# A hybrid block (linear attention, FFN, softmax attention, FFN) on one core: loads ahead, two products moved to ScalarE, weight codes converted early, down projections and softmax reordered

## The chip, the cores and the metric

The kernel runs on 1 core of one Trainium2 chip. The metric is device time in microseconds of one execution; smaller is better. A core has five engines with a queue each: TensorE (PE, matrix products), VectorE (DVE), ScalarE (ACT), GpSimd (POOL) and SyncE (SP, which here issues nearly all DMAs). In the profile PEld is PE's loading of stationary operands.

## The reference

All arithmetic is float32. `x` is 2 x 1024 rows of 512. Four residual sublayers follow each other:

```python
x = x + linear_attention(layernorm(x))   # 4 heads of 128, chunks of 128 rows
x = x + ffn(layernorm(x))
x = x + softmax_attention(layernorm(x))  # one head of 512, W_q, W_k, W_v, W_o
x = x + ffn(layernorm(x))                # the same weights again
```

The FFN's weights are int32 codes: `W = (code - 128) * scale[:, None]`, 1408 hidden units, and its value is `down(silu(gate(x)) * up(x))`.

The linear attention, for each chunk of 128 rows and each head:

```python
k = k / max(norm(k), 1e-12); alpha = sigmoid(x @ Walpha + b); beta = softplus(x @ Wbeta + b)
cla = cumsum(log(alpha + 1e-6))                      # inside the chunk
decay = where(causal, exp(cla - cla.T), 0)
y_local = ((q @ k.T) * beta.T * decay) @ v
y_glob = (q @ state.T) * exp(cla)
kw = k * beta * exp(cla_end - cla)
state = state * exp(cla_end) + v.T @ kw              # carried from chunk to chunk
```

Its output is `y_local + y_glob`.

## The kernel before

**Precision.** Most operands are kept as a pair: a rounded "high" part (format float32r) made by ScalarE and the remainder, the "low" part, made by VectorE (sometimes POOL). This is `split` (lines 83 to 86). A product of two pairs is three matmuls, `mm3` (95 to 98). Matmuls are 128x128 stationary by up to 512 columns; results go to eight PSUM buffers.

**Order.** The program is written as one straight list of instructions. A planner (`schedule_with_timeline_sim`) then places them on the engines by a simulated timeline of its own; the written order is the priority, not the final order. Each engine executes its own list strictly in the order planned. `behind(instructions)` (76 to 81) forbids the planner to place what is inside the block ahead of the given instructions on the same engine. Tiles come from pools; a pool with `bufs=2` has two buffers for a name, and a third use waits until the first is free. The large pool is `slots`, twelve buffers of 8 KB a partition (`slot`), which hold weights, transposed activations and FFN operands in turn.

**Start.** A weight product M = Wq Wk^T of the softmax attention is made in four steps (`weight_product`), while the first four tiles of x (128 rows each) are normed and transposed by PE (`ln_tile`): none at step 0, tile 0 at step 1, tiles 1 and 2 at step 2, tile 3 at step 3. Each tile's load is issued inside `layernorm` (103 to 117). Then Wq, Wk and Wv are loaded through four stage buffers and split (`load_wqkv`).

**Linear attention loop.** For t = 0 to 15: one head of the q projection of four tiles further on (`q_head`), k and v projections of tile t+1 (`kv_tile`), the decay matrix of tile t+1 (`decay`: load a row of cumulated logs broadcast to all partitions, mask on POOL, four exponentials on ACT, L491), then `scores(t)`: transpose k, normalise the next k (`k_norm`, which also makes kw on POOL, L531), decay the state (POOL, L555), add to it, form the output of tile t-1 (`chunk_out`) and the scores of t, multiply with the decay matrix (`at`, L566). Beside this, `fill[t]` holds layer norm steps for later tiles: for the attention's tiles 8 to 15 and for the FFN's first 8 tiles (nm "f"). A step of `ln_steps` is either `ln_norm` (norm a tile, transpose blocks of 32 on VectorE into y) or `ln_move` (four DMAs that put the blocks in place). In the loop's last tiles the operands of a second weight product V = Wv Wo are loaded and split, the product is made, and `combine` forms the seven operands of the first FFN pass.

**FFN.** Gate and up projections are done together as a 2x2 block product with seven multiplications, P1 to P7 (`products`, L304), in 2 passes of 8 tiles, each with 11 steps j of 128 hidden units. The stationary operands of a step are eight 128x256 blocks (`stationary`): gate and up codes and four sums or differences of them. In the very first pass they are made from the codes: load, convert to float on ACT (`codes`, L271), four sums on POOL (287 to 290), and seven of the eight blocks are written to DRAM as `wc`; later passes load them from there. The down codes are converted in the attention loop (`down_weights`). `finish(j)` applies silu and the product and splits the hidden values of tiles 0 and 1 of the pass.

After the 11 steps come eight down projections (i = 0 to 7, 22 matmuls each, L761 and 762). Their stationary operand hs is a pair for each tile, from a pool of two buffers; tile i+1 is split while tile i is multiplied (`h_split`). The result is scaled on VectorE (L763) and the residual is added on POOL (L765; on VectorE only for the very last tile). In the blocks behind, norm steps or `combine` steps for the next pass or stage are taken.

**Softmax attention.** For two batches of 8 tiles: `scores_b(i+1)` (maximum on VectorE L829, its negative nm L832 and L833, exponential on ACT L838), `probs_T(i)` (transpose on VectorE, to DRAM and back in four DMAs, then split into pth and ptl), `out_b(i-1)`. The last tile is transposed on PE instead (ppt, L866). `fill[b][i]` again holds norm and combine steps for the next stage.

Of the kernel before, what the change touches and what calls it, by code (L numbers as in the profile page):

```python
# [22 lines left out]
H = 4  # L23
# [11 lines left out]
def hybrid_block_kernel(ctx: ExitStack, tc: tile.TileContext, a, out):  # L35
# [67 lines left out]
    def layernorm(src, name, tag="xin"):  # L103

        xin = xp.tile([P, D], F32, tag=tag, name=f"xin_{name}")
        nc.sync.dma_start(out=xin, in_=src)
        bn = mp.tile([P, 6], F32, tag="bn", name=f"bn_{name}")
# [6 lines left out]
        nc.gpsimd.tensor_tensor(rs, ve, mhalf, ALU.pow)  # L114
# [4 lines left out]
    def layernorm_T(src, xT, i, name, tag="xin"):  # L119

        xn = layernorm(src, name, tag)
# [19 lines left out]
    wc_d = [dp.tile([P, 7, 256], F32, tag=f"wc_{j}", name=f"wc_{j}") for j in range(KH)]  # L141
# [29 lines left out]
    def spill(pool, tag, ps, dst, name):  # L171
        for m in range(KD):
            hi, lo = (pool.tile([P, 512], F32R, tag=tag, name=f"{name}{m}_{j}") for j in range(2))
            split(hi, lo, ps[m])
            nc.sync.dma_start(out=dst[m][:, 0:512], in_=hi.bitcast(F32))
            nc.sync.dma_start(out=dst[m][:, 512:1024], in_=lo.bitcast(F32))

    lnT, lnY = {}, {}

    def ln_norm(src, nm, st, i):  # L180


        if i == 0:
            lnY[nm, st] = yp.tile([P, 4, KD, ST, 32], F32, tag="y", name=f"y_{nm}{st}")
        t = st * ST + i
        xn = layernorm(src[t], f"{nm}{t}")
# [78 lines left out]
    def codes(pool, tag, dst, src_ap, name):  # L265

        c = pool.tile([P, 512], I32, tag=tag, name=name)
        nc.sync.dma_start(out=c, in_=src_ap)
        if len(dst.shape) == 3:
            c = c.rearrange("p (n c) -> p n c", n=2)  # L270
        nc.scalar.activation(dst, c, AF.Identity, bias=zero)  # L271

    def down_weights(sp, j):
        c = sp.tile([P, 512], F32, tag="stg", name=f"cf{j}")
        codes(sp, "stg", c, a["wd"][j], f"cd{j}")
        nc.sync.dma_start(out=wd_d[j], in_=c)

    def stationary(j, name, fresh=None):
# [3 lines left out]
        if fresh:  # L282
            a21, a11, s1, s2, s3, a12, s4, a22 = (w[:, n] for n in range(8))
            codes(*fresh, w[:, 1:6:4], a["wgu"][j][:, 0:512], f"cg{name}_{j}")
            codes(*fresh, w[:, 0:8:7], a["wgu"][j][:, 512:1024], f"cu{name}_{j}")
            f = lambda x: x.bitcast(F32)
# [4 lines left out]
            nc.sync.dma_start(out=wc_d[j], in_=f(w[:, 1:8]))  # L291
        else:
            nc.sync.dma_start(out=w[:, 1:8].bitcast(F32), in_=wc_d[j])
# [728 lines left out]
```

## Time and profile before

| | us |
|---|---|
| median of 3 runs | 997.01 (995.41 to 999.16) |
| the profiled execution, its own time | 995.43 |
| its span, first to last instruction | 993.7 |
| PE busy (4450 matmuls) | 955.3, 96% |
| DVE busy | 681.8, 69% |
| ACT busy | 374.2, 38% |
| POOL busy | 269.0, 27% |
| DMA: 160.06 MB | mean 161 GB/s |
| mean granted PE clock | 0.991 |

The profile is one execution seen by the hardware profiler. Busy time of PE is a pipelined figure, so an engine at 96% is waiting for at least the rest. Its groups name the line of the kernel, the engine, the output and input tiles with buffer numbers left out, the shape, and what ended the engine's idle time before them. Stages in the span: start to 30 us; attention loop to 252; first FFN, passes to 325 and 455 with their down projections after them, to 500; softmax attention to 760; second FFN to the end.

### The profile page before, as it was taken

Reading aid. Unit: us, or ns where it says so; the run is one execution under the profiler, and the core shown is the slowest. Engines: PE = TensorE matmul, PEld = TensorE weight load, DVE = VectorE, ACT = ScalarE, POOL = GpSimd, SP = SyncE. Lnnn points to the kernel's source line nnn. Section 1 sums busy time; section 2 is a strip of 40 time slices with the busy share of each in tenths; the row PEclk is TensorE's granted clock in tenths of the full one; section 3 lists DMA queues with packets and bytes.
Section 4 is the critical chain, followed back from the end, with each engine's and each line's share of the span. In section 5 each row is a group of like instructions: output and inputs, shape, how many; then the busy total and the mean of one; then the engine's idle time right before and its main releaser. Section 6 shows DMA issues by size and latency. Waiting matters only on the chain.

```text
span 993.7 us, 13137 instructions
## 1 busy us (share of the span) xinstructions
PE 955.3 (96%) x4450; PEld 786.8 (79%) x4450; DVE 681.8 (69%) x1294; ACT 374.2 (38%) x719; POOL 269.0 (27%) x345
## 2 busy tenths in 40 slices
PE   8999999988898999999999999999997999999998
PEld 6788888877776777887888888888876888788877
DVE  7666858779876699786526556356667775976665
ACT  4653334233665433443222223222223443444421
POOL 4442314253634133212200411205501111321122
PEclk9999999999999999999999999999998999999999
DMA  8536364564797555652704767328668762464112
GB/s 271 200 104 174 124 156 140 142 180 158 253 350 229 148 202 205 185 146 75 264 22 88 163 162 168 98 64 190 165 151 271 250 175 44 152 235 153 38 53 96
DMA packets 219250, 160.06 MB, mean 161 GB/s; under 512 B 154992, under 2 KB 170672, under 8 KB 219184
## 3 DMA queue, kind: packets, MB, share of 16 engines
q1 hardware_dynamic: 217136, 155.03, 52.3%
q0 software_dynamic: 2048, 4.20, 2.0%
q8 instruction: 35, 0.57, 0.2%
q14 instruction: 31, 0.25, 0.1%
HBM read 102.66 MB, written 41.84 MB: 145 GB/s over the span
## 4 chain that ended last, share of the span: by engine, by line
PE 56%; DVE 2%; SPq 2%; DMA 1%; ACT 1%; issue 1%; POOL 0%; ACTq 0%; DVEq 0%
PE pZg L304 4%; PE pXg L304 4%; PE pVg L304 4%; PE pog L762 4%; PE pog L761 4%; PE psc L96 3%; PE psc L98 3%; PE pob L96 3%; PE psc L97 3%; PE pob L97 3%; PE pob L98 3%; PE pYg L304 2%; PE pof L762 2%; PE pof L761 2%; PE pqb L97 1%; PE pqb L96 1%
## 5 line engine op out<-in xcount | busy, mean ns | idle before, releaser
L762 PE MATMUL pof<-wdf,hsf 128*128 128x512 f32 x176 | 68.3, 392 | 4.3 <-DVE hsf L86 4.3
L762 PE MATMUL pog<-wdg,hsg 128*128 128x512 f32 (+1 forms) x187 | 69.0, 378 | 3.0 <-DVE hsg L86 3.0
L761 PE MATMUL pog<-wdg,hsg 128*128 128x512 f32 (+1 forms) x187 | 69.1, 378 | 0.0
L761 PE MATMUL pof<-wdf,hsf 128*128 128x512 f32 x176 | 68.1, 391 | 0.0
L96 PE MATMUL pob<-vh,pth 128*128 128x512 f32 x128 | 50.8, 397 | 0.0
L96 PE MATMUL psc<-xh_b,qh 128*128 128x512 f32 x128 | 50.5, 395 | 0.0
L98 PE MATMUL psc<-xh_b,ql 128*128 128x512 f32 x128 | 50.5, 395 | 0.0
L97 PE MATMUL psc<-xT_b,qh 128*128 128x512 f32 x128 | 50.5, 394 | 0.0
L97 PE MATMUL pob<-vl,pth 128*128 128x512 f32 x128 | 50.5, 394 | 0.0
L98 PE MATMUL pob<-vh,ptl 128*128 128x512 f32 x128 | 50.4, 394 | 0.0
L304 PE MATMUL pXf<-B_f,wcf 128*128 128x512 f32 x176 | 47.0, 395 | 3.3 <-ACT u2f L729 2.2
L86 POOL TENSOR_TENSOR hsg<-sgg,hsg 128x128 fp32r<-128x128 f32 x40 | 17.6, 460 | 117.6 <-ACT hsg L85 95.4
L304 PE MATMUL pVf<-T_f,wcf 128*128 128x512 f32 x176 | 46.6, 391 | 1.4 <-DVE upf L735 0.7
L304 PE MATMUL pXg<-B_g,wcg 128*128 128x512 f32 x176 | 47.2, 389 | 0.0
L304 PE MATMUL pVg<-T_g,wcg 128*128 128x512 f32 x176 | 46.7, 389 | 0.0
L85 ACT CAST pth<-ptl 128x512 fp32r<-128x512 f32 x30 | 17.1, 619 | 75.9 <-DMA ptl<-p 64.0
L765 POOL TENSOR_TENSOR xrf<-of,xrf 128x512 f32<-128x512 f32 x16 | 25.0, 1562 | 75.3 <-DVE of L763 61.4
L838 ACT ACTIVATE pe<-psc,nm 128x512 f32<-128x512 f32 x32 | 21.7, 684 | 58.6 <-DVE nm L833 58.6
L762 PEld LDWEIGHTS pog<-wdg,hsg 128*128 128x128 f32 x187 | 35.1, 188 | 10.0 <-DVE hsg L86 3.6
L762 PEld LDWEIGHTS pof<-wdf,hsf 128*128 128x128 f32 x176 | 33.1, 188 | 12.6 <-DVE hsf L86 5.8
L304 PEld LDWEIGHTS pXf<-B_f,wcf 128*128 128x128 f32 x176 | 32.3, 188 | 12.8 <-ACT u2f L729 4.0
L765 POOL TENSOR_TENSOR xrg<-og,xrg 128x512 f32<-128x512 f32 x15 | 24.4, 1624 | 61.5 <-DVE og L763 48.7
(288 smaller groups left out, 2667.7 us busy)
## 6 DMA issues: line engine op xcount, KB each, us to landing
wcg<-wc SPq DMA_DIRECT2D x22, 896.0 KB, 5.8
wc<-wcf SPq DMA_DIRECT2D x11, 896.0 KB, 4.5
wcf<-wc SPq DMA_DIRECT2D x11, 896.0 KB, 4.8
p<-py SPq DMA_DIRECT2D x15, 512.0 KB, 3.0
ptl<-p SPq DMA_DIRECT2D x60, 128.0 KB, 3.0
xin_a<-in_x SPq DMA_DIRECT2D x16, 256.0 KB, 4.6
xra<-in_x SPq DMA_DIRECT2D x16, 256.0 KB, 3.0
row<-cl SPq DMA_DIRECT2D x16, 256.0 KB, 4.0
```

Of the source, the lines that this page charges most:

```text
L85: c = nc.scalar.copy(hi, src)
L86: return c.ins, (eng or nc.vector).tensor_tensor(lo, src, hi.bitcast(F32), ALU.subtract).ins
L96: nc.tensor.matmul(ps, lhs_hi, rhs_hi, start=first, stop=False)
L97: nc.tensor.matmul(ps, lhs_hi, rhs_lo, start=False, stop=False)
L98: return nc.tensor.matmul(ps, lhs_lo, rhs_hi, start=False, stop=last).ins
L304: nc.tensor.matmul(ps, w[:, m, k * P : (k + 1) * P], o[:, s, k, :], start=first and k == 0 and s == 0, stop=k == 1 and s == 1, skip_group_ ...
L761: nc.tensor.matmul(ps, hs[i][:, 0, j], wd[j][:, ds], start=j == 0, stop=False)
L762: nc.tensor.matmul(ps, hs[i][:, 1, j], wd[j][:, ds], start=False, stop=j == KH - 1)
L765: add.tensor_tensor(xr[:, ds], o[:, ds], xr[:, ds], ALU.add)
L838: nc.scalar.activation(pe[:, s * 512 : (s + 1) * 512], pS[s], AF.Exp, bias=nm, scale=SC, accum_out=rs[:, s : s + 1],).ins
```

## The change

**Loads ahead.** `load_x` is taken out of `layernorm`. The first four tiles are loaded at product steps 0 and 1, tiles 0 and 1 are normed at step 1, tiles 2 and 3 at step 2. Wq is loaded in step 2, into the buffer of y, and split from there, behind the latest inverse root on POOL. `ln_norm` loads the tile after its own too, within a group of four. The broadcast rows of `decay` are loaded up to two tiles ahead (`load_row`), and `decay(t+1)` comes after `scores(t)`.

**To ScalarE.** kw and the decayed state are made by four ACT instructions each, one a head, instead of one POOL instruction.

**Codes.** All 33 blocks of codes are loaded, converted on ACT and stored during tiles 0 to 11 (`convert`, called three times a tile; each call starts one load and converts and stores an earlier block). `stationary` then loads four blocks of float codes and forms (first pass) or loads (later) the other four; formed ones are stored. The first two stationaries are formed after the loop.

**Spread.** The norm steps for the FFN come earlier (tiles 6 to 11 instead of 6 to 12); the V operands at tiles 13, 14, 14 and 15 instead of 12 to 15; combine steps three each at tiles 12, 13 and 14, and the last three in the FFN's first step, behind the last spill of V. In the first FFN pass norm steps are taken in twos.

**Down projections and softmax.** hs of tile 2 gets two buffers of `slots` and is split around the last `finish`; from then on tile i+2 is split while tile i is multiplied. The residual add goes to VectorE. In `probs_T` the splits are put behind the latest exponential (ACT) and reciprocal (DVE).

```diff
-        nc.gpsimd.tensor_tensor(rs, ve, mhalf, ALU.pow)
+        rsqrt[:] = [nc.gpsimd.tensor_tensor(rs, ve, mhalf, ALU.pow).ins]
...
     def ln_norm(src, nm, st, i):
+        t = st * ST + i
+        for n in range(t, min(t + 2, st * ST + ST)):
+            if (nm, n) not in lnX:
+                lnX[nm, n] = load_x(src[n], f"{nm}{n}")
...
+    def load_codes(sp, n, j):
+        c = sp.tile([P, 512], F32, tag="stg", name=f"c{n}{j}")
+        src = {"g": a["wgu"][j][:, 0:512], "u": a["wgu"][j][:, 512:1024], "d": a["wd"][j]}[n]
+        nc.sync.dma_start(out=c.bitcast(I32), in_=src)
+        return n, j, c
+
+    def store_codes(n, j, c):
+        nc.scalar.activation(c, c.bitcast(I32), AF.Identity, bias=zero)
+        if n == "d":
+            nc.sync.dma_start(out=wd_d[j], in_=c)
+        else:
+            dst = wa_d[j][:, 1:3] if n == "g" else wa_d[j][:, 0:4:3]
+            nc.sync.dma_start(out=dst, in_=c.rearrange("p (n c) -> p n c", n=2))
+
+    def stationary(j, name, form=False):
         w = slot(f"wc{name}_{j}").rearrange("p (n c) -> p n c", n=8)
+        nc.sync.dma_start(out=f(w[:, 0:4]), in_=wa_d[j])
+        if form:
+            a21, a11, a12, a22, s1, s2, s3, s4 = (w[:, n] for n in range(8))
...
+            nc.sync.dma_start(out=ws_d[j], in_=f(w[:, 4:8]))
         else:
-            nc.sync.dma_start(out=w[:, 1:8].bitcast(F32), in_=wc_d[j])
+            nc.sync.dma_start(out=f(w[:, 4:8]), in_=ws_d[j])
...
-                weighted = nc.gpsimd.tensor_tensor(kw, kf, s2.unsqueeze(2).to_broadcast([P, H, P]), ALU.mult)
+                for h in range(H):
+                    weighted = nc.scalar.activation(kw[:, h, :], kf[:, h, :], AF.Copy, scale=s2[:, h : h + 1])
...
-                    nc.gpsimd.tensor_tensor(
-                        old, sta[t], ec[:, 2, i, :].unsqueeze(2).to_broadcast([P, H, P]), ALU.mult
-                    )
+                    for h in range(H):
+                        nc.scalar.activation(old[:, h, :], sta[t][:, h, :], AF.Copy, scale=ec[:, 2, i, h : h + 1])
...
+            if k < 2:
+                xs += [load_x(xa[t], f"a{t}", "xres" if t > 1 else "xin") for t in (2 * k, 2 * k + 1)]
+            if k == 2:
+                staged = yp.tile([P, 4, KD, ST, 32], F32, tag="y", name="y_Wq")
+                staged = staged.rearrange("p k a b c -> p k (a b c)")
+                for m in range(KD):
+                    wq_loaded = nc.sync.dma_start(out=staged[:, m], in_=a["Wq"][m * P : (m + 1) * P, :]).ins
             pm, end = next(prep)
             with behind((end, loads[-1][2])):
-                for t in ((), (0,), (1, 2), (3,))[k]:
+                for t in ((), (0, 1), (2, 3), ())[k]:
                     ln_tile(t)
...
-            (x1, "f", 0, (6, 7, 8, 9, 9, 9, 10, 10)),
-            (x1, "f", 1, (10, 10, 11, 11, 11, 11, 12, 12)),
+            (x1, "f", 0, (6, 6, 7, 7, 7, 7, 8, 8)),
+            (x1, "f", 1, (9, 9, 10, 10, 10, 10, 11, 11)),
...
+        def convert(t):
+            if t < 12 and taken:
+                if items:
+                    taken.append(load_codes(sp, *items.pop(0)))
+                store_codes(*taken.pop(0))
+
         for t in range(NT):
+            convert(t)
             if t + 4 < NT:
                 q_head(*divmod(t + 4, ST))
+            load_row(t + 1)
+            if (t + 2) % ST:
+                load_row(t + 2)
             if t + 1 < NT:
                 kv_tile(t + 1)
+            convert(t)
+            weighed = scores(t)
+            if t + 1 < NT:
                 decay(t + 1)
-            scores(t)
-            with behind(normed.get(t + 1, ())):
+            with behind(normed.get(t + 1, (weighed,))):
                 for step in fill[t]:
                     step()
...
+                for n in {NT - 3: (0,), NT - 2: (1, 2), NT - 1: (3,)}.get(t, ()):
+                    loads.append(product_operands(sp, a["WvT"], a["Wo"], "V", n))
+                for n in range(3 if t >= NT - 4 and t < NT - 1 else 0):
                     moving.pop(0)()
+                convert(t)
...
+        wcs = [stationary(n, "f0", True) for n in range(2)]
         chunk_out(NT - 1)
-        spill(a3, "state", next(prep)[0], vo_d, "V")
+        spilled = spill(a3, "state", next(prep)[0], vo_d, "V")
...
+                        if i == 2:
+                            two = [slot(f"hs{nm}{pr}_{i}{n}") for n in "hl"]
+                            hs[i] = [x[:, 0 : KH * P].rearrange("p (j c) -> p j c", j=KH) for x in two]
...
+                    with behind(behind_first if first and j < 2 else ()):
+                        while moving:
+                            moving.pop(0)()
+                        plan = (0, 2, 2, 2, 2, 0, 2, 2, 2, 0, 2) if first else (1, 1, 1, 1, 2, 2, 1, 1, 1, 1, 2)
+                        for _ in range(plan[j] if early else 0):
+                            early.pop(0)()
...
+                h_split(2, slice(0, KH - 1), ha[:, 0, 0 : KH - 1], None)
                 done = finish(*begun)
+                h_split(2, KH - 1, ha[:, 0, KH - 1], None)
...
-                    if 1 <= i < 2 * ST - 1:
-                        n = i + 1
+                    if 1 <= i < 2 * ST - 2:
+                        n = i + 2
...
-                        add = nc.vector if last else nc.gpsimd
-                        add.tensor_tensor(xr[:, ds], o[:, ds], xr[:, ds], ALU.add)
+                        nc.vector.tensor_tensor(xr[:, ds], o[:, ds], xr[:, ds], ALU.add)
...
-            for s in range(2):
-                ks = slice(s * 4, s * 4 + 4)
-                split(hi[:, ks], lo[:, ks], raw[:, ks])
+            with behind(last):
+                for s in range(2):
+                    ks = slice(s * 4, s * 4 + 4)
+                    split(hi[:, ks], lo[:, ks], raw[:, ks])
```

## The prediction

> **What bounds the kernel now.** I read the page first: part 1 says that TensorE (PE) is busy for 955.3 of 993.7 us, so no engine can be relieved to any profit unless PE waits for it. Then I cut the span into the kernel's stages and asked for busy time, granted clock and DMA share of each (columns: PE, PEld, DVE, ACT, POOL busy us with instruction counts, clock, DMA share, GB/s).
>
> ```profile
> 0.00:30.00 30.00, 26.03 (x111) 20.19 (x112) 22.00 (x52) 14.37 (x26) 13.82 (x24) 0.94 0.87 284
> 30.00:200.00 170.00, 169.44 (x962) 144.80 (x961) 120.09 (x301) 72.12 (x154) 55.64 (x64) 1.00 0.50 144
> 200.00:252.00 52.00, 43.40 (x250) 37.78 (x249) 46.22 (x99) 18.45 (x35) 25.03 (x25) 0.93 0.56 165
> 252.00:325.00 73.00, 66.39 (x278) 50.61 (x277) 54.60 (x103) 43.47 (x81) 35.76 (x46) 1.00 0.85 284
> 325.00:388.00 63.00, 59.45 (x258) 47.88 (x257) 50.58 (x75) 22.70 (x35) 16.58 (x14) 1.00 0.55 175
> ...
> 455.00:500.00 45.00, 43.53 (x192) 35.62 (x191) 27.04 (x30) 14.03 (x22) 11.64 (x8) 1.00 0.54 196
> ...
> 740.00:760.00 20.00, 13.21 (x53) 10.77 (x52) 19.28 (x37) 6.72 (x12) 1.83 (x3) 0.83 0.68 194
> ...
> 840.00:876.00 36.00, 34.53 (x152) 28.16 (x151) 29.93 (x29) 14.54 (x19) 9.76 (x6) 1.00 0.40 132
> ```
>
> The linear attention's steady part (30 to 200 us), the second halves of both FFN passes and the softmax attention up to 740 us are full: nothing is to be had there. All that can be won is PE's idle time in seven places: start 4.0 us, attention's tail 8.6, first FFN pass 6.6, down projections 3.5 + 1.5 + 1.5 + about 1.5 (at 957.6), softmax's end 6.8; about 34 us. A low clock adds to it: 0.06 of 30 us, 0.07 of 52, 0.17 of 20, that is 1.8 + 3.6 + 3.4 = 8.8 us. The ceiling of any reordering is thus some 43 us.
>
> PE's waits name what ends last in each (columns: total, times, longest):
>
> ```profile
> PE ppt L866 <- ACT pe L838: 6.8, 1, 6.8
> PE pof L762 <- DVE hsf L86: 4.3, 4, 1.5
> PE pl L578 <- DVE at L566: 3.2, 1, 3.2
> PE pd L549 <- POOL kw L531: 3.1, 2, 2.2
> PE pog L762 <- DVE hsg L86: 3.0, 2, 1.5
> PE pkT L540 <- DVE kb L524: 2.3, 3, 0.9
> PE pXf L304 <- ACT u2f L729: 2.2, 3, 0.8
> PE pab L365 <- ACT xh_a L85: 1.7, 1, 1.7
> ```
>
> The timeline shows why the down projections stall (the third tile's operand at 957 us, and a later tile's at 355 us):
>
> ```profile
> 957.47 1.27 POOL L765 TENSOR_TENSOR xrg<-og,xrg 128x512 f32<-128x512 f32 x1 [9.69 <-issue]
> 957.57 1.99 DVE L86 TENSOR_TENSOR hsg<-hag,hsg 128x768 fp32r<-128x768 f32 x1 [0.23 <-ACT hsg L85]
> ...
> 355.60 0.94 DVE L86 TENSOR_TENSOR hsf<-hbf,hsf 128x768 fp32r<-128x768 f32 x1
> ```
>
> The same instruction takes 0.94 us alone and 1.99 us when a POOL add runs beside it; and it can only start once tile 0's matmuls have freed one of the two hs buffers.
>
> **What the Trainium skill says.** "SBUF — State Buffer", section "Who interferes with whom": VectorE with two SBUF inputs and GpSimd reading SBUF exclude each other for the whole instruction, while ScalarE has ports of its own. The trace agrees: 1.05 us longer, about the length of the add. "TensorE: Matmul & The Clock Gate", section "Part 1: The HAM clock gate": an idle window of about 3.4 us halves the clock for at least another. The trace agrees in kind: the clock falls to half after the waits near 20, 206, 246 and 745 us, not after the 1.5 us ones; here waits of 2.2 and 3.2 us were already enough. For the price of a new operation, "ScalarE: Activation LUTs", section "What ACT_TABLE_LOAD costs": 280 ns and 0.833 ns an element with a pointer operand, less 93 ns back to back, so an estimate of 0.29 us for 128 columns; the trace's own row has four decays (L491, 128x128) in 1.28 us, 0.32 each, which I use.
>
> **The change, part by part**, against the profiled execution (995.4 us, span 993.7).
>
> *Start.* Four x tiles are loaded by name ahead and normed at product steps 1 and 2 instead of 1 to 3; Wq goes to the idle y buffer instead of waiting for stage buffers. Now tile 3's transposes end the M product (18.3 us) and PE then waits 1.7 + 0.9 us for its halves, after which 3.4 us run at half clock. With tile 3 done a step earlier both waits go. Eight loads of 256 KB now stand on SP's queue about the M operands, at 0.87 DMA share; a 1 us delay of an M operand is possible. Gain 2.6 + 1.7, less 1: **3.3** (0 to 4.5).
>
> *Steady loop.* kw (15 tiles) and the decayed state (14 tiles) leave POOL (1.13 and 1.04 us each) for ScalarE, four instructions of 0.32 each, 1.28 us: 29 x 1.28 = 37 us more ACT. The 22 gate and up code conversions (0.72 us) leave the FFN for tiles 0 to 11: 15.8 us. Of this some 13 x 2.56 + 15.8 = 49 us falls in 30 to 200, on top of 72.1: 121 of 170 us, 71%. ACT is in order, so kT, qT and the squares may stand behind a group of four. PE has projections to run meanwhile. SP gets 22 loads and 22 stores more at 0.33 to 0.43 us, some 1.5 us in a tile of 12 us, and DMA 11.5 MB more, 68 GB/s on 144; the rows, now loaded up to two tiles ahead, are out of reach of that. A store waits for its conversion, and behind it wait x loads and x1 stores. From nothing to 1.5 us a tile; I take a **loss of 3** in all.
>
> *Attention's tail.* Here DVE is 46.2 of 52 us busy: it is the bound, not PE. What goes: f's norms of tiles 4 to 7, each 0.68 + 0.17 + 0.14 + 0.55 + 0.65 = 2.2 us, move a tile or so earlier, so about two tiles' worth leaves the window (4.4); three of the twelve combining steps go behind the last spill (about 3.5); with kw and the decayed state off POOL, port blocks like the 2.06 us for a 1.21 us B_f split at 227 us shrink (say 3 us). Forming two stationaries (8 x 0.8 us of POOL) moves past the loop's end; kw's two waits (3.1) go, for ScalarE is two fifths busy here. DVE falls to about 35 of 52. That removes perhaps two thirds of 8.6 and one of two slow-clock windows: **7** (3 to 11).
>
> *First FFN pass.* ACT loses 22 conversions that stood in its queue ahead of u2 and waited for code loads (8.1 + 2.3 us by the waits). Instead weights come by DMA: load 512 and store 512 KB a step against 512 and 896 before, on queues 0.85 busy. POOL still forms 4 x 0.8 = 3.2 us a step of 6.3. Norm steps are two at a time, same total. PE's waits here were u2, sg, wcf: **5** of 6.6 go (2 to 6.5).
>
> *Down projections.* hs of tile 2 gets two slots of its own and is split before or right after the last finish; each later tile is split two ahead. The start waits have no cause left. The residual add goes to DVE: 0.68 us more a tile of 5 us, against a 1 us block removed. If no block was there, DVE in 340 to 388 rises from 39.8 to at most 45.2 of 48: still covered, but the second pass's operands, combined there on DVE, would come later (0.9 us wait at 386.7 now). Of 8.0 us idle: **6.5** (3 to 8).
>
> *Softmax's end.* The splits of tile 14's probabilities are put behind tile 15's exponentials. Before, ACT took pth at 748.1 when its DMA landed, DVE took ptl between the two nm steps (747.9 and 750.6), and the exponentials came at 751.1. Without these, nm is done near 748.1 and exponentials follow T_g's casts, at 748 to 749.5: 2.3 us. What is late next is DVE: the maxima stand behind combining steps until 744.9, though scores ended at 739.7, and that stays. One slow-clock window of two may go, 1.7: **4** (0 to 9). Elsewhere in the stage the new wait only orders ACT and DVE, which are a quarter and a half busy.
>
> Sum: 3.3 + 7 + 5 + 6.5 + 4 - 3 = 22.8; 995.4 - 22.8 = 972.6. The runs' median is 997.0, 1.6 above the profiled one; I say **973**.
>
> **Rivals.** (a) *DVE stays the bound in the tail, and maxima stay late:* DVE there does 7 us a tile beside 9.5 us of PE work, plus combining; the order on a FIFO, not the sum, ended the 3.2 us wait for `at`. Then tail, softmax and start give 3 + 0 + 2 instead of 14.3: 995.4 - 13.5 = 982. Spoken for by DVE's 19.3 of 20 at 740. (b) *Nearly all idle time goes*, since removing one wait also removes the clock's fall: 34 + 8.8 less an irreducible 1.2 at start and some 4 is 37.6: 958. Against it: seven separate causes. (c) *Gains and new waits cancel:* the bounds' low ends sum to 8, against a loop loss of 5 to 12: 992 to 999. (d) *Slower: ACT's queue paces the loop.* Place: kT behind four kw, four decayed-state and four decay instructions (3.8 us), before scores; PE's small matmuls then wait in each tile. Price: 2.5 us in 13 tiles is 32 us, 995.4 - 25.8 + 32 = 1002. It decides from 2.4 us a tile on. For it: ACT at 71% in order; against it: ACT ends 30% idle and projections fill 8 us of each tile.
>
> **How the numbers follow.** My forecast (965 to 982) 0.50; (a) 0.19; (b) 0.14; (c) 0.07; (d) 0.10. The range 957 to 992 leaves out (d), most of (c) and the part of (b) below 957, about 0.2. About 0.5% (5 us) can be told from no change. Faster 0.83, same 0.07, slower 0.10.
>
> **What would show it.** Right: no PE wait for hs; PE idle from 200 to 252 at 3 us or so; no `pab` wait; ACT near 120 us in the loop with PE still full. Wrong: PE waits on kT or kw in each tile (d), on `at` and `kb` as before (a), or a wait for pX at the second pass's start, DVE being full.

## The result, and the profile after

| | before | after |
|---|---|---|
| median, us | 997.37 (995.41 to 999.16, 4 runs) | 1026.18 (1023.74 to 1026.95, 4 runs) |
| span of the profiled execution, us | 993.7 | 1024.4 |
| mean granted PE clock | 0.991 | 0.976 |
| DMA, MB | 160.06 | 171.61 |

The change made the kernel slower: ratio 1.0283, 95% interval [1.0262, 1.0304]. The prediction, 973 with a range of 957 to 992, was wrong in sign. The first part of the page after has the same 4450 matmuls and a little more time in them:

```profile
span 1024.4 us, 13264 instructions
PE 959.9 (94%) x4450; PEld 789.7 (77%) x4450; DVE 676.2 (66%) x1325; ACT 405.5 (40%) x823; POOL 188.8 (18%) x288
```

PE's busy time grew by 4.6 us and the span by 30.7, so PE waits more. The same stage windows as before say where (columns as in the prediction):

```profile
0.00:30.00 30.00, 27.55 (x127) 21.74 (x128) 25.02 (x54) 16.37 (x30) 16.82 (x26) 1.00 0.86 292
30.00:200.00 170.00, 137.04 (x723) 114.44 (x722) 94.40 (x240) 87.28 (x202) 28.61 (x37) 0.90 0.64 187
```

The start is what was forecast: 1.5 us more of PE's work in 30 us and no half clock. The steady loop, in which "nothing is to be had", is where the time went: PE idles 33.0 us of 170 instead of 0.6, and the clock is 0.90 instead of 1.00. ScalarE did not run out of time: it is busy 87 of 170 us, less than the 121 predicted, because the loop is stretched and fewer tiles fit in the window. PE's waits name what ended last (columns: total, times, longest):

```profile
PE pab L376 <- ACT xh_a L85: 23.6, 2, 12.0
PE pS L581 <- ACT kT L560: 9.0, 6, 2.8
PE ppt L922 <- ACT pe L894: 6.1, 1, 6.1
PE pXf L314 <- DMA wcf<-wa: 4.7, 2, 3.1
PE pkT L558 <- DVE kb L541: 3.9, 2, 2.7
```

Two single waits of 12 us for `xh_a`, the rounded half of the attention's next four tiles, make most of it. The waits for `hs` (7.3 us over both FFNs in the lines of before) and for `kw` have gone, as predicted. The softmax's wait (`ppt`) has hardly moved: 6.1 after 6.8.

ScalarE's list around the first of the two waits shows why a cast of 0.5 us came 12 us late. Before, the casts stood directly behind kT and the squares, and the decay groups came after them:

```profile
91.47 0.59 ACT L542 COPY kT<-pkT 128x512 f32<-128x512 f32 x1 [5.25 <-PE pkT L540]
91.95 0.63 ACT L516 ACTIVATE sq<-sWk 128x512 f32<-128x512 f32 x1
92.48 2.16 ACT L85 CAST xh_a<-xT_a 128x512 fp32r<-128x512 f32 x4
94.55 0.72 ACT L271 ACTIVATE cf<-cd,zero 128x512 f32<-128x512 int32 x1
96.41 1.28 ACT L491 ACTIVATE dec<-row,ncl 128x128 f32<-128x128 f32 x4 [1.13 <-POOL row L479]
```

After, the same casts stand last (the bracket gives the engine's idle time ahead of the instruction and what ended it):

```profile
96.03 0.59 ACT L560 COPY kT<-pkT 128x512 f32<-128x512 f32 x1 [2.74 <-PE pkT L558]
96.51 0.63 ACT L533 ACTIVATE sq<-sWk 128x512 f32<-128x512 f32 x1
99.69 1.28 ACT L574 ACTIVATE sdec<-state,ec 128x128 f32<-128x128 f32 x4 [2.54 <-DVE state L575]
106.16 1.28 ACT L498 ACTIVATE dec<-row,ncl 128x128 f32<-128x128 f32 x4 [5.20 <-POOL row L486]
107.35 0.70 ACT L282 ACTIVATE cg<-cg,zero 128x512 f32<-128x512 int32 x1
107.96 1.26 ACT L498 ACTIVATE dec<-row,ncl 128x128 f32<-128x128 f32 x4
109.13 0.70 ACT L282 ACTIVATE cu<-cu,zero 128x512 f32<-128x512 int32 x1
109.74 1.26 ACT L549 ACTIVATE kw<-sWk,s 128x128 f32<-128x128 f32 x4
110.91 2.16 ACT L85 CAST xh_a<-xT_a 128x512 fp32r<-128x512 f32 x4
```

The reason is a line that the change did not touch. `normed[t] += (weighted.ins,)` (L550) adds kw to the instructions that `behind(normed...)` (L693) sets ahead of the norm steps of `fill[t]`, and an instruction is held back on the engine of the one it must follow. While kw was made by GpSimd, that bound GpSimd. Now that kw is made by ScalarE, no cast of a norm step may stand ahead of it there. kw(t+1) in turn stands behind decay groups, which wait for a broadcast row, and behind conversions of codes, which wait for loads. The Trainium skill says of such lists, in "Perfetto Trace Analysis", section "Tensor Engine Instruction (MATMUL, LD_WEIGHTS)", that "ACT/DVE/GPSIMD are strict FIFO"; the list above agrees: ScalarE stood idle for 5.20 us with four casts behind the waiting group.

The row came late as well. SyncE's list ahead of it, and the mask on GpSimd that waited for it:

```profile
90.68 5.32 SPq L205 DMA_DIRECT2D xT_a<-y_a  x8
96.76 0.38 SPq L449 DMA_DIRECT2D cl<-clr  x1
98.60 0.82 SPq L506 DMA_DIRECT2D row<-cl  x2
105.49 0.64 POOL L486 TENSOR_SCALAR_AFFINE_SELECT row<-row 128x512 f32<-128x512 f32 x1 [13.01 <-DMA row<-cl]
```

The cumulated logs were stored at 96.8, behind eight moves of 0.66 us each, and the row's load followed at 98.6. A row can be loaded ahead only as far as its logs exist: for the first tile of a group of four they are written in the tile before it, so "out of reach" did not hold for tiles 4, 8 and 12.

### The profile page after: what moved, and what is told of

Same layout as the page of the kernel before. It is cut to its first block, busy times and chain, and to the rows that moved or that the text cites. A ratio compares the mean times of both kernels' runs of the same rounds, so it can differ in the third digit from the quotient of the medians.

```text
span 1024.4 us, 13264 instructions
## 1 busy us (share of the span) xinstructions
PE 959.9 (94%) x4450; PEld 789.7 (77%) x4450; DVE 676.2 (66%) x1325; ACT 405.5 (40%) x823; POOL 188.8 (18%) x288
## 2 busy tenths in 40 slices
DMA packets 230164, 171.61 MB, mean 168 GB/s; under 512 B 156048, under 2 KB 174544, under 8 KB 230096
## 4 chain that ended last, share of the span: by engine, by line
PE 64%; DMA 16%; DVE 9%; ACT 3%; issue 3%; SPq 2%; POOL 2%; DVEq 0%; ACTq 0%; POOLq 0%
PE pog L817 4%; PE pog L816 4%; PE pXg L314 4%; PE pZg L314 4%; PE pVg L314 4%; PE pZf L314 3%; PE pXf L314 3%; PE pVf L314 3%; PE pof L816 2%; PE pof L817 2%; PE psc L96 2%; PE psc L98 2%; PE psc L97 2%; DMA cu<-in_wgu 2%; PE pob L98 2%
## 5 line engine op out<-in xcount | busy, mean ns | idle before, releaser
L816 PE MATMUL pog<-wdg,hsg 128*128 128x512 f32 (+1 forms) x165 | 60.3, 375 | 0.0
L817 PE MATMUL pog<-wdg,hsg 128*128 128x512 f32 (+1 forms) x165 | 60.2, 375 | 0.0
L817 PE MATMUL pof<-wdf,hsf 128*128 128x512 f32 x154 | 59.5, 390 | 0.0
L816 PE MATMUL pof<-wdf,hsf 128*128 128x512 f32 x154 | 59.5, 389 | 0.0
L117 POOL TENSOR_TENSOR rs_b<-ve_b,mhalf 128x1 f32<-128x1 f32 x16 | 9.8, 615 | 218.4 <-DVE ve_b L115 200.5
L314 PEld LDWEIGHTS pVf<-T_f,wcf 128*128 128x128 f32 x176 | 32.7, 188 | 12.1 <-DVE ve_f L115 1.9
L885 DVE TENSOR_REDUCE mx<-psc 128x1 f32<-128x512 f32 x32 | 21.8, 685 | 27.0 <-PE psc L98 26.8
L314 PEld LDWEIGHTS pXg<-B_g,wcg 128*128 128x128 f32 x176 | 33.0, 188 | 6.9
L314 PEld LDWEIGHTS pVg<-T_g,wcg 128*128 128x128 f32 x176 | 33.0, 188 | 6.9
```

Source lines behind the costliest of these rows:

```text
L117: rsqrt[:] = [nc.gpsimd.tensor_tensor(rs, ve, mhalf, ALU.pow).ins]
L314: nc.tensor.matmul(ps, w[:, m, k * P : (k + 1) * P], o[:, s, k, :], start=first and k == 0 and s == 0, stop=k == 1 and s == 1, skip_group_ ...
L816: nc.tensor.matmul(ps, hs[i][0][:, j], wd[j][:, ds], start=j == 0, stop=False)
L817: nc.tensor.matmul(ps, hs[i][1][:, j], wd[j][:, ds], start=False, stop=j == KH - 1)
L885: nc.vector.tensor_reduce(mx[:, s : s + 1], ps, AX.X, ALU.max)
```

## The experiments

Three causes stood against each other: the ordering edge that came along with kw; the new handling of the codes, through ScalarE's queue (a conversion waits for its load), SyncE's queue (a store waits for its conversion) or the transfers themselves; and the rows with `decay` behind `scores`. Rival (d) of the prediction, ScalarE's added work itself, is a fourth. Each ratio is to the kernel before, measured beside it, with its 95% interval.

**Taking the edge away, and what else changed, from the kernel after.**

```diff
-                normed[t] += (weighted.ins,)
```

> Changed kernel with one line less: kw (now on ScalarE) is no longer among the instructions behind which the norm and split steps of a tile are put. Theory A (the ordering edge: moving kw to ScalarE silently puts the splits of the next x group behind kw, and so behind the decay exponentials that wait for rows): both 12 us waits of pab for xh_a go, with 3 us of low clock, 1026 falls to about 999. Rival B (SP's queue, crowded by code loads and stores, brings rows late): the waits move to scores or stay, 1020 or more. Rival C (ScalarE's load itself): under 5 us better, 1022.

Measured 1004.84 (1002.47 to 1007.42), ratio 1.0056 [1.0033, 1.0078]: 21.3 us less by one line that computes nothing. PE's waits:

```profile
PE pS L580 <- ACT kT L559: 9.2, 4, 3.3
...
PE pab L376 <- ACT xh_a L85: 0.9, 2, 0.5
```

The wait for the casts fell from 23.6 to 0.9 us; the one for kT, 9.2, stayed. The edge is shown, and it is not all. (Taking the line out also lets the planner order the rest of the lists anew; the pairs below tell whether that matters.)

**kw and the decayed state on GpSimd again**, the edge left in place (it then binds GpSimd, as before):

```diff
-                for h in range(H):
-                    weighted = nc.scalar.activation(kw[:, h, :], kf[:, h, :], AF.Copy, scale=s2[:, h : h + 1])
+                weighted = nc.gpsimd.tensor_tensor(kw, kf, s2.unsqueeze(2).to_broadcast([P, H, P]), ALU.mult)
```

> Changed kernel with kw and the decayed state on POOL again. Theory A: as without the ordering edge, about 999, and the waits of scores for kT (9 us) shrink as well, to 995. Rival B: the row waits remain, 1018 or more. Rival C: most of the whole loss goes, 995, and it is several us better than the run that takes only the ordering away.

Measured 1007.17 (1006.70 to 1008.09), ratio 1.0077 [1.0057, 1.0096], with 2.2 us of waits for `xh_a` and 11.7 for kT. Taking the 29 groups off ScalarE, which takes the edge off it too, gives no more than taking off the edge alone, so ScalarE's added work is not what costs.

**Codes handled as before**, the rest as after (`convert` out; `codes`, `down_weights` and the old `stationary` back):

```diff
-            convert(t)
...
+                if 1 <= t <= KH:
+                    down_weights(sp, t - 1)
...
-        wcs = [stationary(n, "f0", True) for n in range(2)]
+        wcs = [stationary(n, "f0", (sp, "stg")) for n in range(2)]
```

> Changed kernel with the weight codes handled as before (down codes only in the loop, gate and up codes converted in the FFN's first pass). Theory A: the order on ScalarE stays, but rows come sooner, so the two waits shrink from 12 to some 5 us each: 1012. Rival B: both waits go, and the waits for kT with them: 995 to 999. Rival C: 15 us of conversions less in the loop, 1018.

Measured 998.44 (994.76 to 1005.68, 20 runs), ratio 1.0001 [0.9985, 1.0017]: 27.7 us less than after. The waits for kT are gone; those for the casts remain, at 13.5 us (two, the longest 7.1).

**Rows and `decay` as before**, the rest as after:

```diff
-            row = rowa.pop(t)
+            row = tl("row", t)
+            nc.sync.dma_start(
...
-            if t + 1 < NT:
-                decay(t + 1)
```

> Changed kernel with the decay rows loaded where they are used and the decay made before the scores, as before. Theory A and rival B: no large difference, 1022 to 1030, for neither the ordering edge nor the crowd on SP's queue is touched. A rival D (the new place of the decay, behind the scores, is what makes ScalarE late): 1005 or less.

Measured 1022.25 (1021.71 to 1022.74), ratio 1.0229 [1.0212, 1.0246], with 22.0 us of waits for the casts: 3.9 us less than after. The rows' new place is at most a small part, and the traces do not put even that in the loop: from PE's transposes of k (pkT) of tile 0 to those of tile 12 this kernel takes 189.9 us, the kernel after 186.0.

**Edge and codes together**, the two edits above in one kernel:

> Changed kernel with the codes handled as before and kw no longer among the instructions behind which the next group's splits are put. Theory A with code traffic as its second half: the two 7 us waits for xh_a that are left with the codes as before go, with 3 us of low clock: 998 less 17, 981. If the waits had another cause (rival B's queue alone, or DMA time): 992 or more.

Measured 980.53 (979.43 to 981.51), ratio 0.9811 [0.9788, 0.9835]. The four kernels make a square:

| us | codes as after | codes as before | codes cost |
|---|---|---|---|
| with the edge | 1026.18 | 998.44 | 27.7 |
| without | 1004.84 | 980.53 | 24.3 |
| edge costs | 21.3 | 17.9 | |

The kernel before, measured beside each, had medians of 997.37, 999.07 and 998.20, so a difference in this square is good to some 2 us. One stretch of the traces gives the same square more sharply: from tile 0's transposes of k to tile 12's it takes 186.0 us with both, 165.2 with the edge alone, 169.4 with the codes alone and 148.7 with neither (148.0 in the kernel before). There the edge costs 16.6 and 16.5 us, the codes 20.8 and 20.7. Four kernels with the loop of the fifth, this one included, lie between 148.2 and 148.7.

Both causes act nearly alone; together they cost 45.7 us by the medians, and what is left of the change is a gain of 17.7 (998.20, measured beside it, less 980.53). Its loop:

```profile
30.00:200.00 170.00, 168.21 (x952) 143.25 (x951) 120.86 (x313) 97.02 (x242) 36.26 (x47) 1.00 0.53 153
```

ScalarE has more to do in the loop than in the kernel after (97.0 us against 87.3) and PE idles 1.8 us there. Its own waits between 40 and 200 us tell the kernels apart. After:

```profile
ACT cg L282 <- DMA cg<-in_wgu: 21.8, 8, 5.6
ACT cu L282 <- DMA cu<-in_wgu: 19.6, 9, 4.1
ACT dec L498 <- POOL row L486: 12.1, 3, 5.2
```

Without edge and new codes:

```profile
ACT kT L556 <- PE pkT L554: 26.8, 10, 5.2
ACT kw L546 <- DVE s L543: 10.6, 5, 3.6
ACT dec L495 <- POOL row L483: 8.9, 6, 3.1
```

In the first, ScalarE waits 41.4 us for code loads with everything else behind it; in the second it waits mostly for PE, which is how an engine with time to spare looks.

**Which queue carries the codes' cost?** Two kernels without the edge: the conversions moved to GpSimd, and the codes' DMAs moved to GpSimd with the conversions left on ScalarE.

```diff
-        nc.scalar.activation(c, c.bitcast(I32), AF.Identity, bias=zero)
+        nc.gpsimd.tensor_scalar(c, c.bitcast(I32), -ZERO_POINT, None, ALU.add)
```

> Changed kernel without the added order (1004.8), with the codes converted on POOL instead of ScalarE; code loads and stores are as many as before. If conversions that wait for their loads at the head of ScalarE's queue make kT late (9 us of waits in the loop): these go, 993. If the crowd on SP's queue or DMA time is the link by itself: 1002 or more, POOL's row masks being late instead.

Measured 1011.00 (1010.63 to 1011.50), ratio 1.0125 [1.0103, 1.0148]. The waits for kT went, as they should if the conversions on ScalarE made them. The trace without the edge shows the largest of its four such waits being made; PE, which needs this kT, then stood idle for 3.31 us:

```profile
132.45 0.72 ACT L282 ACTIVATE cg<-cg,zero 128x512 f32<-128x512 int32 x1 [3.13 <-DMA cg<-in_wgu]
133.08 0.57 ACT L559 COPY kT<-pkT 128x512 f32<-128x512 f32 x1
```

But not all four are of this kind: the one of 2.46 us at 217 us comes after the last conversion, behind a decay group that waited 8.01 us for its row. And with the conversions on GpSimd a wait for code loads, with others behind it, is in that queue. First PE's wait there, then two of GpSimd's between 40 and 200 us:

```profile
PE pab L376 <- ACT xh_a L85: 14.5, 2, 9.2
```

```profile
POOL row L486 <- DMA row<-cl: 24.3, 8, 14.0
POOL cg L282 <- DMA cg<-in_wgu: 9.1, 5, 3.2
```

One row waited 14 us, and the casts were late by way of sixteen moves of their operand issued in one run from 97 us on. The second kernel:

```diff
-        nc.sync.dma_start(out=c.bitcast(I32), in_=src)
+        nc.gpsimd.dma_start(out=c.bitcast(I32), in_=src)
...
-            nc.sync.dma_start(out=wd_d[j], in_=c)
+            nc.gpsimd.dma_start(out=wd_d[j], in_=c)
```

> The kernel after without the ordering edge, with the loads and the stores of all 33 code blocks issued by GpSimd instead of SyncE; conversions stay on ScalarE. It stands beside 1004.8 (the same with SyncE) and 980.5 (the same with the codes handled as before). If SyncE's queue, in which a store waits for its conversion and x loads, rows and the other loads stand behind it, is most of the 24 us between them, the time is 984 to 992. If it is ScalarE's queue, in which a conversion waits for its load, or the transfers' own time, the time stays at 1000 to 1008, and TensorE's waits for kT stay near 9 us. GpSimd then has waiting DMA issues in its own queue, ahead of the mask of the decay matrix: if those waits come last, the time is above 1008.

Measured 1004.47 (1002.66 to 1008.00), ratio 1.0055 [1.0029, 1.0081]: no change from 1004.84. So relieving SyncE's queue in this way gains nothing. ScalarE's waits for code loads are no shorter in this kernel, 32.6 us against 27.8 with the DMAs on SyncE:

```profile
ACT cg L282 <- DMA cg<-in_wgu: 16.8, 6, 5.8
ACT cu L282 <- DMA cu<-in_wgu: 15.8, 9, 4.6
```

PE's waits for kT fell to 3.9 us there and those for the casts rose to 11.6: whichever queue holds the loads, stores and conversions, something that PE needs stands behind them.

**The move to ScalarE alone**, with neither edge nor new codes: the second kernel's edit on top of the fifth.

> The kernel with neither the ordering edge nor the new handling of the codes (980.5), with the product kw and the decayed state put back on GpSimd. It prices the move to ScalarE alone, without what it dragged along. If GpSimd's longer instructions only cost what they did in the pair of experiments with the new codes (2.3 us), the time is 982 to 984; if ports shared with VectorE matter in the attention's tail as the prediction said (3 us), and the waits for kw (3.1 us) come back, it is 985 to 988; if the move has no worth of its own, 980 to 981.

Measured 984.52 (979.92 to 989.09), ratio 0.9860 [0.9821, 0.9898]; the interval overlaps that of the fifth, so the move's worth, 4.0 us by the medians and 2.3 in the pair with the new codes (1007.17 against 1004.84), isn't told from nothing by either pair. From tile 12's transposes of k to the first product of the FFN this kernel takes 40.9 us, against 39.0 in the fifth and 48.5 before: most of the tail's gain comes without the move.

**The other way round: parts added to the kernel before.** First kw and the decayed state on ScalarE alone, with the edge:

> Kernel before with only kw and the decayed state moved to ScalarE, the ordering as it comes. Theory A: the casts of the next x group now stand behind kw and two decay groups, which wait for rows: two waits of 5 to 7 us and low clock, 997 + 14 = 1011. If the edge bites only together with the other parts of the change (code traffic, late decay): 995 to 999.

Measured 1011.12 (1004.30 to 1014.19), ratio 1.0108 [1.0063, 1.0153], with 15.1 us of waits for `xh_a`, the longest 7.0. The edge costs without any other part of the change: from tile 0 to tile 12 this kernel takes 164.4 us, 16.4 more than the kernel before. Three pairs of kernels give the edge 16.4 to 16.6 us there, so an accident of the planner's new order is unlikely.

Then the down projections alone (hs two ahead, residual add on VectorE; the buffers for tile 2 are not shown):

```diff
+                h_split(2, slice(0, KH - 1), ha[:, 0, 0 : KH - 1], None)
                 done = finish(*begun)
+                h_split(2, KH - 1, ha[:, 0, KH - 1], None)
...
-                    if 1 <= i < 2 * ST - 1:
-                        n = i + 1
+                    if 1 <= i < 2 * ST - 2:
+                        n = i + 2
...
-                        add = nc.vector if last else nc.gpsimd
-                        add.tensor_tensor(xr[:, ds], o[:, ds], xr[:, ds], ALU.add)
+                        nc.vector.tensor_tensor(xr[:, ds], o[:, ds], xr[:, ds], ALU.add)
```

> Kernel before with only the down projection's part of the change: tile 2's hs in two slots, splits two ahead, residual add on VectorE. By the prediction's step: 6.5 us below the kernel before, 991, with no wait for hs left. If VectorE's extra 0.68 us a tile made the next pass late: 997 or more.

Measured 997.32 (993.20 to 1000.63, 20 runs), ratio 0.9983 [0.9971, 0.9996]: a miss. The waits for hs are gone, but one of a similar size is new where the second FFN pass begins. The window from 375 to 400 us, before and with this part:

```profile
375.00:400.00 25.00, 24.31 (x108) 19.77 (x107) 23.19 (x43) 8.25 (x17) 8.32 (x11) 1.00 0.66 233
```

```profile
375.00:400.00 25.00, 21.70 (x81) 16.79 (x80) 21.87 (x37) 8.20 (x11) 5.32 (x4) 0.86 0.65 225
```

PE waits less on its way to the pass (busy 46.9 of the 48 us from 340 on, against 44.4), and VectorE, which now adds the residuals too and is full at 22 of 25 us, has not combined the pass's operands. The second FFN keeps its gain: from its first down projection to the end it takes 155.8 us, against 159.6. With the norm steps of the first pass in twos, VectorE has that work behind it in time:

```diff
-                    for _ in range((1, 1, 1, 1, 2, 2, 1, 1, 1, 1, 2)[j] if early else 0):
+                    plan = (0, 2, 2, 2, 2, 0, 2, 2, 2, 0, 2) if nm == "f" and pr == 0 else (1, 1, 1, 1, 2, 2, 1, 1, 1, 1, 2)
+                    for _ in range(plan[j] if early else 0):
```

> Kernel before with the down projection's part and the norm steps of the first FFN pass in twos (16 of 16 taken in the pass instead of 14). If the 6 us that the down projection's part gained were given back because the combining of the second pass's operands, queued on VectorE with the moved residual add, came late: with two steps fewer left over it starts a tile sooner, the loss at the second pass's start (6.6 us) falls to 2, and the time to 993. If something else gave it back: 997 as with the down part alone.

Measured 995.17 (989.16 to 997.85, 11 runs), ratio 0.9954 [0.9930, 0.9979]. The loss at the second pass is gone: from the first down projection to the softmax attention 175.3 us, against 182.9 with the down projections alone. But a wait of 7.8 us came in the first pass for a converted weight block, whose load stood behind the moves of two norm steps, and that pass takes 86.9 us to the first down projection instead of 80.3.

**Taking the pairs out again**, from the fifth kernel:

```diff
-                        plan = (0, 2, 2, 2, 2, 0, 2, 2, 2, 0, 2) if first else (1, 1, 1, 1, 2, 2, 1, 1, 1, 1, 2)
+                        plan = (1, 1, 1, 1, 2, 2, 1, 1, 1, 1, 2)
```

> As the run with codes as before and the order taken away, and in the first FFN pass the norm steps are taken one at a time as before, not in twos. If eight moves in a row on SP's queue (8 x 0.66 us) are what holds the weight load of a step back (3.7 us wait, 5 us with the slower matmuls around it): 4 to 5 us below that run, 977. If it is DMA time or POOL's sums: no change, 981.

Measured 982.79 (981.38 to 985.71), ratio 0.9839 [0.9806, 0.9871]: a miss. The first pass waits less, but PE is busy 21.41 of 25 us from 360 on, against 24.15. The old plan takes 14 steps in a pass and 16 are to be done; two are left for the time in which VectorE must combine.

**The softmax's end.** From the fifth kernel, combine steps moved from the sixth tile to the seventh to bring the maxima forward, and, in another, the splits no longer put behind the exponentials:

```diff
-            fill[1][(5, 5, 5, 5, 5, 6, 6, 6, 6, 7, 7, 7)[n]].append(step)
+            fill[1][(5, 5, 5, 5, 5, 7, 7, 7, 7, 7, 7, 7)[n]].append(step)
```

> The run without early codes and without the added order (980.5), with seven of the twelve combining steps of the last FFN moved from tile 6 to tile 7 of the second batch, that is behind the last exponentials. If VectorE's queue, which holds combining steps ahead of the last maxima, makes the 6 us wait for the exponentials: the wait falls to 3 us or less and one window of low clock goes, 975. If the operands are then late for the last FFN instead: 980 or more.

Measured 987.19 (984.82 to 988.55), ratio 0.9884 [0.9853, 0.9915]: a miss, 6.7 us slower than the fifth. PE's waits from 720 to 770 us:

```profile
PE pXg L311 <- DMA wcg<-wc: 10.3, 1, 10.3
PE ppt L908 <- ACT pe L880: 2.2, 1, 2.2
```

The wait for the exponentials falls from 6.0 to 2.2, and the next one grows to 10.3.

```diff
-            with behind(last):
-                for s in range(2):
+            for s in range(2):
```

> The run without early codes and without the added order (980.5), with the splits of the transposed probabilities not put behind the exponentials. The prediction's step gave this part 4 us: 984.5 without it. The profile after says that casts on ScalarE took the place of the removed wait, so that it is worth 0 to 2: 980 to 982.5.

Measured 978.97 (977.74 to 982.23), ratio 0.9809 [0.9781, 0.9838]: the order of the splits is worth nothing that can be measured. This is the fastest kernel by its median, within the spread of the fifth.

## Why the prediction was wrong, point by point

**The failed step is "Steady loop".** It counted the moved instructions by their length (37 us of ScalarE) and took "a **loss of 3** in all" from "nothing to 1.5 us a tile". From tile 0 to tile 12 the loop grew by 38.0 us (148.0 to 186.0), and the two causes in it cost 45.7 us of the whole. Two things in that step were off, and a third is open.

- *An order by engine.* `weighted` became an instruction of another engine, and the edge that names it with it: 21.3 us (17.9 without the new codes, both by removing that one line). The prediction's waits show L531, the line above the edge (L532 before, L550 after), but it asked only who would wait for kw, not what kw was a fence for.
- *Waiting, not working.* A conversion was priced at 0.72 us. At the head of an in-order queue it costs its wait for the load as well, 41.4 us in all between 40 and 200 us (27.8 without the edge), and what stands behind it pays. The step said that "a store waits for its conversion, and behind it wait x loads", and priced that within the 3. The codes cost 24.3 us without the edge, and 20.7 of them arise between tile 0 and tile 12 (169.4 against 148.7).
- *The rows* were called "out of reach"; at the start of a group of four they weren't. What that cost is not shown: loading them as before, with `decay` in its old place, gave back 3.9 us, but not between tile 0 and tile 12.

**Rival (d)** named ScalarE's queue as the slower case, with 1002 and a chance of 0.10. Its engine was right, its place and price not: it expected 2.5 us for kT in each of 13 tiles, for the length of the groups; the trace has six waits for kT, 9.0 us, and two of 12 for the casts. With all 29 groups on ScalarE and neither edge nor new codes the loop takes 148.7 us from tile 0 to tile 12, against 148.0 before: the length of the groups alone does next to nothing.

**Start, 3.3:** right for the first 30 us: 1.5 us more PE work and the clock at 1.00 instead of 0.94 (1.8 by the prediction's own reckoning). By tile 0 the fifth kernel still has 2.7 us of it; the kernel after has 0.1.

**Attention's tail, 7:** more than forecast, and in part for another cause. The tail from tile 12's transposes to the FFN's first product, before and in the fifth kernel:

```profile
203.40:251.90 48.50, 40.40 (x237) 35.62 (x237) 45.23 (x97) 16.90 (x30) 22.48 (x22) 0.93 0.55 162
```

```profile
201.40:240.40 39.00, 39.00 (x250) 34.85 (x249) 32.95 (x62) 23.22 (x49) 13.32 (x12) 1.00 0.54 166
```

It is 9.5 us shorter, and PE is full. With kw and the decayed state on GpSimd it takes 40.9, so the share put on ports, "say 3 us", and on the waits for kw can be some 1.9 us at most. The rest came with a VectorE that is busy 33 us there instead of 45: earlier norm steps and later combining. Which of the two did it was not tried. Rival (a), in which VectorE stays the bound here, is out for the fifth kernel.

**First FFN pass, 5:** the pass got longer instead. From its first product to the first down projection it takes 86.6 us in the kernel after and 84.2 in the fifth, against 80.4 before. In the kernel after PE waits there for weights by DMA instead of for conversions. Here the load of a block left SyncE's queue behind eight moves, since norm steps come in twos:

```profile
327.44 5.29 SPq L205 DMA_DIRECT2D xT_f<-y_f  x8
332.84 0.56 SPq L294 DMA_DIRECT2D wcf<-wa  x1
337.23 1.73 PE L314 MATMUL pXf<-B_f,wcf 128*128 128x512 f32 x4 [3.06 <-DMA wcf<-wa]
```

"Norm steps are two at a time, same total" was the error: the total is the same, the queue in front of a load is twice as long. The two kernels with the new down projections show its price alone, 80.3 us without the twos and 86.9 with them.

**Down projections, 6.5:** the mechanism was right, the waits for hs went, and the second FFN gained 3.8 us in the fifth kernel. In the first FFN the price that the prediction named, "the second pass's operands, combined there on DVE, would come later", was seen but given no term of its own; alone, this part gave nearly all of its gain back (997.32 against 998.20 beside it). With the norm steps in twos it gains 3.3 us (998.46 - 995.17), an interval that overlaps the other. What the twos give behind the first pass they take in it: from its first product to the softmax attention the first FFN takes 261.8 us before, 262.2 after and 260.7 in the fifth kernel.

**Softmax's end, 4:** nothing. The prediction said of the maxima "and that stays", and it did. The rows of after, in order of time:

```profile
778.39 0.68 DVE L885 TENSOR_REDUCE mx<-psc 128x1 f32<-128x512 f32 x1
782.10 1.99 ACT L85 CAST T_g<-xT_g 128x1024 fp32r<-128x1024 f32 x2 [7.50 <-DVE xT_g L253]
782.84 0.14 DVE L889 TENSOR_SCALAR nm<-nm 128x1 f32<-128x1 f32 x1
784.00 0.68 ACT L894 ACTIVATE pe<-psc,nm 128x512 f32<-128x512 f32 x1
```

Without the splits in the way, the casts of T_g start just ahead of the last step of the negative maximum, and the exponentials wait for their end. The prediction has them follow these casts; what it left out is that the casts themselves wait for VectorE, here until 782.1 us.

**The sum.** The span divided at starts of PE's instructions, each row from the mark of the row above, in us (fifth: without edge and new codes):

| stretch | before | after | fifth | gain forecast | gain in the fifth |
|---|---|---|---|---|---|
| to tile 0's transposes of k | 55.4 | 55.3 | 52.7 | 3.3 | 2.7 |
| to tile 12's transposes of k | 148.0 | 186.0 | 148.7 | -3 | -0.7 |
| to the first FFN's first product | 48.5 | 43.1 | 39.0 | 7 | 9.5 |
| to its first down projection | 80.4 | 86.6 | 84.2 | 5 | -3.8 |
| to the first softmax scores | 181.4 | 175.6 | 176.5 | part of 6.5 | 4.9 |
| to the second FFN's first product | 252.4 | 253.5 | 253.3 | 4 | -0.9 |
| to its first down projection | 68.0 | 68.0 | 68.0 | 0 | 0.0 |
| to the end | 159.6 | 156.2 | 155.8 | part of 6.5 | 3.8 |

The first row is not told to better than some 2 us: the kernel before and two that differ from it only in the FFNs reach tile 0 at 55.4, 56.2 and 57.6. What was read off PE's idle time was about right for the attention's start and tail and for the second FFN, 12.2 and 3.8 us; the first FFN and the softmax attention as wholes gave nothing. That the fifth kernel's gain comes near the 20.8 forecast for start, tail, down projections and softmax is in part luck, since the tail gave 2.5 more than its share. What turned the sign was the price of putting new waits into in-order queues in a stage that had no slack.

**What stays open.** How the 24.3 us of the codes divide between the queues, the four stage buffers and the added 11.5 MB was not settled; moving the DMAs or the conversions alone changed the place of the waits and brought no gain. The traces point at the buffers. A code load goes into the buffer of an earlier block, and its issue waited for that block's store. Without the edge, between 40 and 200 us (L277 issues the loads):

```profile
SPq L277 <- DMA wa<-cu: 16.2, 10, 3.5
SPq L277 <- DMA wa<-cg: 15.3, 8, 3.4
```

With the stores of down codes it is 35.1 us, 38.6 with the conversions on GpSimd and, in GpSimd's own queue, 30.3 with the DMAs there. So a load waits for an earlier block's store, that store for its conversion, and that conversion for its own load, whichever queues they stand in. That this ring is the cause is not shown; a kernel with more stage buffers was not tried.

## What to carry to other kernels

When an instruction moves to another engine, look up every order that names it: a fence that was harmless on one engine can hold back unrelated work on the next. Price an instruction in an in-order queue by its longest wait and by what stands behind it, not by its length; in a stage where PE is full, a conversion that waits for its load makes other work late in whatever queue it stands; here it gained nothing to move it to another engine. And a gain read from one wait holds only as far as the engine that is late next: two of the parts here removed their wait and moved it a few microseconds on.

## What the runs showed that was not expected

- Eight small moves, issued in one run, take 5.3 us of SyncE's time (0.66 each), more than the 0.33 to 0.43 us that the prediction took for an issue; anything behind them is late by that much.
- GpSimd takes 1.5 us to convert 128x512 codes (11 in 16.4 us), ScalarE 0.70: moving conversions to the idle engine doubled their length.
